# A planner that counts changes of TensorE's tile division and table loads, and orders ready TensorE steps by them

## The chip, the cores and the metric

The kernel runs on one core of a Trainium2 chip. Its engines work side by side, each through its own list of instructions in order, and wait for each other through semaphores: TensorE (PE in the profile, its weight loads PEld), VectorE (DVE), ScalarE (ACT), GpSimd (POOL) and SyncE (SP), which issues most DMAs. The metric is the device time of one execution in microseconds (us). Before the change it is 3449.53 us, the median of three runs (3448.21 to 3455.52).

## What is computed

Six residual blocks act on x, 4 sequences of 1024 tokens with 128 features, all in float32:

```python
x = x + 0.5 * ffn0(layernorm(x))      # 128 -> 512, exact GELU, -> 128
x = x + attn0(layernorm(x))           # 16 heads of 8, scores from squared distances, softmax over 1024
x = x + 0.5 * ffn0(layernorm(x))
x = x + 0.5 * ffn1(layernorm(x))      # two layers, see below
x = x + attn1(layernorm(x))           # 16 heads of 64, causal softmax
x = x + 0.5 * ffn1(layernorm(x))
```

Each layer of `ffn1` shifts half of the features by one token, makes queries, keys and values for 8 heads of 64, normalises and rotates queries and keys, attends locally (each window of 64 tokens sees itself and the window before it), projects and adds to the residual; then it shifts again, takes a layer norm, and runs a gated feed-forward (a value half times GELU of a gate half). The two calls of `ffn1` share their weights.

## The kernel before

**Two passes.** The kernel isn't written as one instruction stream. Its code registers some thousands of small *steps* with `plan.at(t, f, ...)`, each a function with one to a few dozen instructions and a first guess `t` of its time. In a first pass the class `Plan` runs all steps in recording mode: `issue` notes for each instruction its engine and an estimated cost, and `touch` derives which step has to follow which. `order` then simulates the engines with these costs and brings the steps into one order. In the second pass the steps run again in this order and emit the real instructions. Each engine gets its instructions in exactly the planned order (`issue` adds a dependence on the engine's instruction before); the times of the plan themselves leave no trace on the chip, which runs each list as fast as its waits allow. Since one helper line, 223, emits everything, all rows of the profile say L223, and shapes tell the steps apart.

**How the plan is made.** `cost` (276) gives each instruction a duration by engine, operation and size. A TensorE product in float32 streams its columns four times (`4 * n / 2400` us), other types once, with a lower bound by type. A product with at most 64 weight columns whose output starts below the first partition counts 0.04 us. `order` (343) keeps for each engine a list `future` of steps whose predecessors are planned and a heap `ready`, sorted by due time `p`. It takes the engine that can start first and its ready step with the smallest `p`, gives it buffers if it needs them (`places`), and lays its instructions on the engines' clocks: 0.22 us (`X_LAT`) from one engine to another, 0.12 between two VectorE instructions of a step, fixed costs for SP's DMAs. At first `p` is the written time `t`. `latest` (502) then plans backward and finds how late each step may start; this becomes `p`, and `best_order` (554) repeats this six times and keeps the order that ended earliest by its own reckoning. `prepare` (306) puts a barrier between groups of steps that need different ScalarE tables (Exp or GELU). SBUF addresses come from the written times; which of a tag's buffers or PSUM slots a step gets is settled in `order`.

**The steps that matter here**, with the part of TensorE's 128 x 128 array that their products use (rows x weight columns):

- First attention (`attn0`, 807): `score` (975) has two products of 64 x 128 in bfloat16, 512 wide; `exp` (984) is one ScalarE instruction over 128 x 1024; `weigh` (988), for two exponentials, has four products of 128 x 9 with 512 columns to stream, placed beside each other in the array. Preparation of the next batch (transposes, projections) is 128 x 128. There are 512 scores and exponentials and 256 weighings; the exponentials have six buffers, the scores two PSUM slots.
- Causal attention (`attn1`, 1078): `score` (1270), transposes, projections use the whole array; `weigh` (1341) has pairs of products of 128 x 64, 256 wide, in 128 steps. The transposed exponentials that it reads have six buffers.
- Local attention (`ffn1`, 1420): `attend` (1644) registers the steps of one *frame*, 128 tokens through one layer's attention; two layers of 32 frames make 64 for each `ffn1`. `score` (1740) starts with two mask products on the whole array and goes on with 16 products of 64 x 64; `weigh` (1791) has 32 of 128 x 64; all else is 128 x 128. Between score and weighing lie a maximum on DVE, exponentials on ACT, a reciprocal on DVE, a multiplication on POOL (`norm_e`, 1778) and transposes on PE (`turn_e`, 1782). Every four frames the next block's tokens are shifted by DMAs. The gated feed-forward of four blocks is gathered between two table changes.

A float32 product counts twice in the profile: it runs as two passes, each with its weight load.

Of the kernel before, what the change touches and what calls it, by code (L numbers as in the profile page):

```python
# [11 lines left out]
FR = mybir.dt.float32r  # L12
# [35 lines left out]
def free_size(x):  # L48
    return math.prod(x.shape[1:])
# [42 lines left out]
class Plan:  # L92
# [6 lines left out]


    X_LAT, LAT, AHEAD = 0.22, {"D": 0.13, "A": 0.09, "G": 0.09, "S": 0.22}, 0.1
    TRIES = 6

    def __init__(self, ctx, tc):
# [116 lines left out]
    def issue(self, engine, name, args, kw):  # L221
        if not self.recording:
            ins = getattr(engine.engine, name)(*args, **kw)  # L223
            prev = self.last.get(engine.key)
            if prev is not None:
                info = mybir.DependencyInfo(mybir.DependencyClass.NoSync, mybir.DependencyReason.DATA)
                self.tc.add_manual_dep(ins.ins, prev, info, reason="order of the plan")
            self.last[engine.key] = ins.ins.name
            return
        out = [kw["out"] if "out" in kw else args[0]] + ([kw["accum_out"]] if "accum_out" in kw else [])  # L230
        ins = [x for x in (*args, *kw.values()) if isinstance(x, bass.AP) and not any(x is o for o in out)]
        banks = {}
        for write, aps in ((False, ins), (True, out)):
            for x in aps:
                b = self.owner.get(x.tensor.name)
                if b is not None:
                    self.touch(b, x, write)
                    if b.space == "P":
                        banks[b] = True
        if name == "activation" and args[2] in (AF.Exp, AF.Gelu):  # L240
            self.cur.table = args[2]
        self.cur.work.append((engine.key, self.cost(engine.key, name, args, kw, out[0], ins), banks))

    def touch(self, b, x, write):
        row = math.prod(x.tensor.shape[1:])
# [27 lines left out]
        if b.users[-1] is not cur:  # L273
            b.users.append(cur)

    def cost(self, key, name, args, kw, out, ins):

        n = free_size(out)
        if key == "P":
            if name == "transpose":  # L280
                return 0.109 if args[1].dtype == F32 else 0.056
            x, w = args[2], args[1]
            if x.dtype == F32:
                t = 4 * free_size(x) / 2400
            else:
                t = max(free_size(x) / 2400, 0.107 if x.dtype == FR else 0.056)
            row = math.prod(out.tensor.shape[1:])
            return 0.04 if free_size(w) <= 64 and out.offset // row else t + 0.004
        if key == "A":
            extra = sum(isinstance(kw.get(z), bass.AP) for z in ("bias", "scale", "accum_out"))  # L290
            return 0.055 + n / 1200 + 0.093 * extra
# [51 lines left out]
    def order(self):  # L343
# [9 lines left out]
            s.left, s.est, s.state, s.behind = len(s.before), 0.0, 0, []  # L353
        free = dict.fromkeys("PADGS", 0.0)
        future, ready = {z: [] for z in "PADGS"}, {z: [] for z in "PADGS"}
        todo, out, dma = [s for s in self.all if not s.left], [], 0.0

        def places(s):

# [64 lines left out]
        while True:  # L424
# [31 lines left out]
                break  # L456
            z = best[1]
            s = self.all[heapq.heappop(ready[z])[1]]
            if s.buffers:
                found = places(s)  # L460
                if found is None:
                    s.state = 0
                    wait(s)
                    continue
                e = max(t for t, _ in found)
                if e > s.est + 1e-9:
                    s.est = e
                    heapq.heappush(future[z], (e, s.p, s.index))
                    continue
                take(s, found)  # L470
            t, before, last = s.est, z, 0.0
            for j, (e, cost, banks) in enumerate(s.work):
                t = max(t, free[e])
                if e != before:
                    t += self.X_LAT
                for b in banks:
# [1583 lines left out]
```

## Time and profile before

| | us |
|---|---|
| median of 3 runs | 3449.53 |
| profiled execution | 3451.22 |
| span of its instructions | 3449.4 |
| granted TensorE clock, mean | 0.96 of full |
| ACT table loads, 18 | 23.1 |

The page cuts the span into 40 slices and gives each engine's busy share in tenths (9 is 90% or more), and below them the granted TensorE clock:

```profile
PE   8999999888787889789999999999998888888868
PEld 6222222766676767567777777777776666667647
DVE  7433240788768687888888888888888797886874
ACT  6999999467667576547667777777776666776753
POOL 1000000276646464433333333333345664664650
PEclk9999999999899999889999999999999999999989
```

The first attention shows as the run of 9s of PE and ACT at the left (slices 2 to 7), the causal attention as PE's run of 9s in the middle (slices 18 to 30), and the two local stages on either side of it, where PE falls to 7 and 8 and the clock drops in places. Busy PE is modelled: the end of a product includes a tail in which the next one already runs.

### The profile page before, as it was taken

Reading aid. Unit: us, or ns where it says so; the run is one execution under the profiler, and the core shown is the slowest. Engines: PE = TensorE matmul, PEld = TensorE weight load, DVE = VectorE, ACT = ScalarE, POOL = GpSimd, SP = SyncE. Lnnn points to the kernel's source line nnn. Section 1 sums busy time; section 2 is a strip of 40 time slices with the busy share of each in tenths; the row PEclk is TensorE's granted clock in tenths of the full one; section 3 lists DMA queues with packets and bytes.
Section 4 is the critical chain, followed back from the end, with each engine's and each line's share of the span. In section 5 each row is a group of like instructions: output and inputs, shape, how many; then the busy total and the mean of one; then the engine's idle time right before and its main releaser. Section 6 shows DMA issues by size and latency. Waiting matters only on the chain.

```text
span 3449.4 us, 76651 instructions
## 1 busy us (share of the span) xinstructions
PE 3066.5 (89%) x27060; PEld 2178.1 (63%) x27060; DVE 2497.1 (72%) x7673; ACT 2424.1 (70%) x6434; POOL 1351.9 (39%) x1483
## 2 busy tenths in 40 slices
PE   8999999888787889789999999999998888888868
PEld 6222222766676767567777777777776666667647
DVE  7433240788768687888888888888888797886874
ACT  6999999467667576547667777777776666776753
POOL 1000000276646464433333333333345664664650
PEclk9999999999899999889999999999999999999989
DMA  1000000122212121122221222222222221222211
GB/s 38 1 1 1 1 3 13 45 60 49 46 35 51 39 51 33 48 63 46 45 51 42 45 48 46 48 49 46 72 54 54 53 47 35 47 48 46 46 36 28
DMA packets 210677, 138.95 MB, mean 40 GB/s; under 512 B 146596, under 2 KB 165880, under 8 KB 210296
## 3 DMA queue, kind: packets, MB, share of 16 engines
q1 hardware_dynamic: 209576, 133.50, 16.9%
q8 instruction: 216, 3.54, 0.4%
q14 instruction: 165, 1.35, 0.1%
q0 software_dynamic: 720, 0.56, 0.1%
HBM read 19.22 MB, written 2.10 MB: 6 GB/s over the span
## 4 chain that ended last, share of the span: by engine, by line
PE 36%; DVE 25%; issue 3%; SPq 3%; DMA 3%; ACT 2%; POOL 2%; DVEq 0%; ACTq 0%; POOLq 0%
PE wordsP L223 36%; DVE wordsS L223 19%; DVE words L223 4%; SPq L223 3%; DMA wordsS<-wordsS 3%; POOL wordsS L223 2%; ACT wordsS L223 1%; ACT words L223 1%; DVE wordsR L223 1%; POOL words L223 1%; DMA wordsS<-c_rot 0%; ACT wordsR L223 0%; DMA words<-words 0%; DVEq L223 0%; ACT L223 0%
## 5 line engine op out<-in xcount | busy, mean ns | idle before, releaser
L223 PE MATMUL wordsP<-wordsS 128*128 128x128 f32 (+8 forms) x12040 | 1686.1, 334 | 271.8 <-POOL wordsS L223 199.2
L223 PEld LDWEIGHTS wordsP<-wordsS 128*128 128x128 f32 (+3 forms) x10248 | 941.7, 147 | 514.3 <-POOL wordsS L223 263.5
L223 ACT ACTIVATE wordsS<-wordsP,wordsS 128x128 f32<-128x128 f32 (+4 forms) x1952 | 915.6, 490 | 371.4 <-PE wordsP L223 201.1
L223 ACT COPY wordsS<-wordsP 128x512 f32<-128x512 f32 (+4 forms) x1040 | 545.5, 537 | 300.1 <-PE wordsP L223 294.4
L223 PE MATMUL wordsP<-wordsR 128*128 128x512 f32 (+2 forms) x2592 | 722.6, 412 | 29.3 <-DVE wordsR L223 10.7
L223 POOL TENSOR_TENSOR wordsS<-wordsS 128x512 f32<-128x512 f32 (+1 forms) x518 | 539.8, 1057 | 516.0 <-DVE wordsS L223 483.4
L223 POOL TENSOR_SCALAR wordsS<-wordsS 128x640 f32<-128x640 f32 (+7 forms) x512 | 382.4, 750 | 683.8 <-DVE wordsS L223 478.6
L223 DVE TENSOR_REDUCE wordsS<-wordsP 128x1 f32<-128x512 f32 (+4 forms) x1024 | 576.2, 581 | 66.5 <-PE wordsP L223 61.0
L223 PE MATMUL wordsP<-wordsS,words 128*64 128x64 f32 (+3 forms) x6216 | 524.8, 300 | 39.5 <-DVE words L223 17.4
L223 PEld LDWEIGHTS wordsP<-wordsR 128*128 128x128 f32 (+1 forms) x2592 | 457.9, 193 | 132.6 <-DVE wordsR L223 13.3
L223 ACT ACTIVATE wordsS<-wordsP 128x1024 f32<-128x1024 f32 x512 | 485.7, 1028 | 23.1 <-PE wordsP L223 20.7
L223 PE MATMUL wordsP<-words 128*128 128x512 f32 (+3 forms) x1540 | 417.7, 377 | 13.2 <-DMA words<-W_vT 10.6
L223 DVE COPY wordsS<-wordsP 128x512 f32<-128x512 f32 (+4 forms) x444 | 238.5, 550 | 209.7 <-PE wordsP L223 206.0
L223 ACT ACTIVATION_READ_ACCUMULATOR wordsS<-wordsP,wordsS 128x1 f32 x1792 | 387.8, 216 | 0.0
L223 DVE TENSOR_TENSOR wordsS<-wordsP,wordsS 128x256 f32<-128x256 f32 (+3 forms) x560 | 253.8, 461 | 162.1 <-PE wordsP L223 129.0
L223 PEld LDWEIGHTS wordsP<-wordsS,words 128*64 128x64 f32 (+2 forms) x5704 | 307.2, 137 | 99.4 <-issue 46.7
L223 PEld LDWEIGHTS <-wordsS 64*128 64x128 bf16 (+1 forms) x1792 | 124.2, 95 | 367.2 <-issue 341.3
L223 PEld LDWEIGHTS wordsP<-words 128*128 128x128 f32 x1540 | 247.3, 192 | 47.5 <-ACT wordsS L223 12.4
L223 ACT ACTIVATE words<-wordsP 128x512 f32<-128x512 f32 x256 | 150.0, 609 | 152.1 <-DVE words L223 74.7
L223 PE MATMUL wordsP<-words,wordsS 64*64 64x128 f32 (+1 forms) x4672 | 234.8, 284 | 24.0 <-DMA words<-words 21.5
L223 DVE TENSOR_TENSOR wordsS<-wordsS 128x1 f32<-128x1 f32 (+4 forms) x1104 | 236.6, 218 | 25.9 <-ACT wordsS L223 13.0
L223 DVE TENSOR_TENSOR words<-wordsP,wordsS 128x256 f32<-128x256 f32 (+1 forms) x448 | 228.9, 529 | 32.1 <-PE wordsP L223 14.7
(55 smaller groups left out, 2441.2 us busy)
## 6 DMA issues: line engine op xcount, KB each, us to landing
words<-words SPq DMA_DIRECT2D x648, 128.0 KB
wordsS<-words SPq DMA_DIRECT2D x88, 128.0 KB
wordsS<-wordsS SPq DMA_DIRECT2D x48, 128.0 KB
wordsS<-wordsS SPq DMA_DIRECT2D x48, 127.0 KB
wordsS<-c_rot SPq DMA_DIRECT2D x16, 256.0 KB
wordsS<-L_attn_x SPq DMA_DIRECT2D x8, 256.0 KB
words<-wordsS SPq DMA_DIRECT2D x16, 128.0 KB
out_dram<-wordsS SPq DMA_DIRECT2D x8, 256.0 KB
```

The lines of the kernel that those rows point to most:

```text
L223: ins = getattr(engine.engine, name)(*args, **kw)
```

## The change

The plan gets another account of what TensorE's work costs, and a rule of choice:

- `mode` gives each TensorE instruction its division of the array: rows and weight columns, each rounded up to 32, 64 or 128, and whether it is a rounded float32 product. `switch` prices a change of rows or columns at 0.1 us (0.2 if one side is 64 x 128 in rounded float32, which no step here has).
- `cost` scales a product by the share of the array that it uses, in place of the 0.04 us for later column tiles; constants per type change a little (a rounded product of 512 from 0.217 to 0.228 us, a float32 product of 128 from 0.217 to 0.222).
- `order` adds the price of a change where the division changes from one instruction to the next, and 1.3 us (`TABLE`) before the first step that needs another table.
- The rule: when the most urgent ready TensorE step would change the division, the plan looks for ready steps that wouldn't, that are due at most 2.0 us (`SLACK`) after it, and that can start by the time it could; if there are any, the most urgent of these goes first.

What the steps do is the same.

```diff
+    SLACK, TABLE = 2.0, 1.3
...
-        self.cur.work.append((engine.key, self.cost(engine.key, name, args, kw, out[0], ins), banks))
+        mode = self.mode(name, args) if engine.key == "P" else None
+        self.cur.work.append((engine.key, self.cost(engine.key, name, args, kw, out[0], ins, mode), banks, mode))
...
-    def cost(self, key, name, args, kw, out, ins):
+    @staticmethod
+    def mode(name, args):
+
+        if name == "transpose":
+            return 128, 128, False
+        tile = lambda n: 32 if n <= 32 else 64 if n <= 64 else 128
+        return tile(args[1].shape[0]), tile(free_size(args[1])), args[1].dtype == FR
+
+    def switch(self, old, new):
+
+        if old is None or old[:2] == new[:2]:
+            return 0.0
+        return 0.2 if any(m == (64, 128, True) for m in (old, new)) else 0.1
+
+    def cost(self, key, name, args, kw, out, ins, mode):
...
-            x, w = args[2], args[1]
+            x = args[2]
             if x.dtype == F32:
-                t = 4 * free_size(x) / 2400
+                t = 4 * free_size(x) / 2400 + 0.009
+            elif x.dtype == FR:
+                t = max(free_size(x) / 2400 + 0.015, 0.112)
             else:
-                t = max(free_size(x) / 2400, 0.107 if x.dtype == FR else 0.056)
-            row = math.prod(out.tensor.shape[1:])
-            return 0.04 if free_size(w) <= 64 and out.offset // row else t + 0.004
+                t = free_size(x) / 2400 + 0.003
+
+            return t * mode[0] * mode[1] / 128**2
...
             s = self.all[heapq.heappop(ready[z])[1]]
+            if z == "P" and self.switch(mode, s.work[0][3]):
+
+                same = [(p, k) for p, k in ready[z] if p <= s.p + self.SLACK and not self.switch(mode, self.all[k].work[0][3])]
+                same = [x for x in same if self.all[x[1]].est <= max(free[z], s.est)]
+                if same:
+                    x = min(same)
+                    ready[z].remove(x)
+                    heapq.heapify(ready[z])
+                    heapq.heappush(ready[z], (s.p, s.index))
+                    s = self.all[x[1]]
...
-            for j, (e, cost, banks) in enumerate(s.work):
+            if s.table is not None and s.table != table:
+                t, table = max(t, free[z]) + self.TABLE, s.table
+            for j, (e, cost, banks, m) in enumerate(s.work):
                 t = max(t, free[e])
+                if e == "P":
+                    t, mode = t + self.switch(mode, m), m
                 if e != before:
                     t += self.X_LAT
```

More of the change, by code (lines that the diff above doesn't have):

```diff
@@ L355, in order @@
         future, ready = {z: [] for z in "PADGS"}, {z: [] for z in "PADGS"}
-        todo, out, dma = [s for s in self.all if not s.left], [], 0.0
+        todo, out, dma, mode, table = [s for s in self.all if not s.left], [], 0.0, None, None
         def places(s):
```

## The prediction

> **What bounds the kernel now.** I read first the page's busy times and slices, then the busy times by stage. The stage borders are mine: they are where the mix of instructions changes (GELU feed-forward, first attention, feed-forward, local attention with gated feed-forward, causal attention, local attention again). The table has one row for each stage: its length, the busy time of each engine with its instruction count, the granted TensorE clock, the DMA share and GB/s.
>
> ```profile
> PE 3066.5 (89%) x27060; PEld 2178.1 (63%) x27060; DVE 2497.1 (72%) x7673; ACT 2424.1 (70%) x6434; POOL 1351.9 (39%) x1483
> ...
> 0.00:85.00 85.00, 68.94 (x513) 59.01 (x514) 67.22 (x306) 57.93 (x113) 13.68 (x18) 1.00 0.15 38
> 85.00:600.00 515.00, 494.31 (x3770) 140.35 (x3769) 162.57 (x483) 491.77 (x526) 3.25 (x3) 1.00 0.01 3
> 600.00:690.00 90.00, 75.82 (x503) 64.20 (x501) 66.67 (x243) 42.80 (x82) 23.70 (x26) 0.92 0.17 44
> 690.00:1485.00 795.00, 648.69 (x7028) 526.07 (x7028) 625.73 (x1948) 514.05 (x1711) 451.04 (x441) 0.92 0.20 45
> 1485.00:2600.00 1115.00, 1086.91 (x7929) 829.77 (x7929) 928.92 (x2760) 785.10 (x2242) 400.10 (x547) 0.99 0.22 51
> 2600.00:3449.00 849.00, 691.87 (x7326) 558.69 (x7323) 645.95 (x1938) 532.49 (x1761) 460.14 (x448) 0.93 0.19 44
> ```
>
> The 89% of PE is an average over stages with different limits. In the first attention ACT works 491.8 of 515 us: it is the bound, and 23 us is all that any order can win there. In the causal attention PE works 1086.9 of 1115: 28 us is open. The two local stages, 1644 us together, have no engine at its limit over the stage, so they are where an order could matter. I looked inside one, at PE in time (start, length, instruction, tiles, count, idle time before) and at two 10 us slices of all engines:
>
> ```profile
> 852.31 0.59 PE L223 MATMUL wordsP<-wordsS 128*128 128x512 bf16 x2
> 852.84 1.10 PE L223 MATMUL wordsP<-words,wordsS 64*64 64x128 f32 x32
> 854.69 0.66 PE L223 MATMUL wordsP<-wordsS 128*128 128x128 f32 x4 [0.75 <-POOL wordsS L223]
> 855.69 1.69 PE L223 MATMUL wordsP<-wordsS 128*128 128x128 f32 x12 [0.34 <-POOL wordsS L223]
> 857.22 0.60 PE L223 MATMUL wordsP<-wordsS,words 128*128 128x128 f32 x4
> 857.69 0.66 PE L223 MATMUL wordsP<-wordsS 128*128 128x128 f32 x4
> 858.28 1.41 PE L223 MATMUL wordsP<-wordsS,words 128*64 128x64 f32 x33
> 859.44 2.34 PE L223 MATMUL wordsP<-wordsR 128*128 128x512 f32 x9
> ...
> 862.25 1.10 PE L223 MATMUL wordsP<-words,wordsS 64*64 64x128 f32 x32
> 864.79 1.43 PE L223 MATMUL wordsP<-wordsS 128*128 128x128 f32 x11 [1.44 <-POOL wordsS L223]
> ...
> 700.00:710.00 10.00, 8.98 (x129) 6.61 (x127) 9.02 (x24) 6.98 (x25) 8.33 (x9) 1.00 0.25 56
> 830.00:840.00 10.00, 9.22 (x129) 7.14 (x131) 9.86 (x32) 7.62 (x29) 7.35 (x9) 1.00 0.12 27
> ```
>
> One frame (128 tokens through the local attention) lasts 862.25 - 852.84 = 9.41 us. PE waits for POOL right after each score; DVE has 9.86 of 10 us filled in the slice at 830 and 9.02 in the slice at 700.
>
> **The change, part by part.** No instruction is added or removed. What changes is the order on each engine, through the plan's costs and one rule. So I ask of each edit how far it brings the plan to the trace, and what an engine could win by it.
>
> *Score of the local attention.* Its 16 products cost the old plan 8 x 0.217 + 8 x 0.04 = 2.06 us (4 x 128 / 2400 + 0.004 for the upper half of the output, 0.04 for the lower). The new one takes a quarter of 0.222 for each: 0.89, with 0.1 on entering and on leaving, 1.09. The row says 1.10 with the tail of the last product. So the old plan put about 1 us of work on PE that isn't there, and the wait of 0.75 to 1.44 us after the score is the trace of it: what was planned next isn't ready. *Weighing*, 32 products of 64 columns: old 16 x (0.111 + 0.04) / 2 = 1.2, new 0.93 + 0.2 = 1.13, trace 859.44 - 858.28 = 1.16. Nothing to win.
>
> What does the freed microsecond bring? It is idle time of PE, which isn't the limit of a frame; DVE is. Where DVE has 9.86 of 10 us the gain is nothing. Where it has 9.02, as in the first layer, at most the 0.84 us of difference per frame. There are 2 stages x 32 such frames. Ends: 64 x 0.8 = 51 us gained, or a loss (rivals). The slice shows the wait, not whether another order removes it, since what PE waits for is POOL's result of the same frame, a chain that the change leaves as long as it is. I take about a quarter, 0.22 us: **-14 us**.
>
> The long holes between blocks of four frames stay. In 790 to 800 us PE is busy 1.75 us and DVE 4.47; the waits of that stage give POOL 134.5 us behind the DMAs of the token shift. Neither SP's costs nor POOL's are touched, and the order around them is free to shift either way.
>
> *Score and weighing of the first attention.* For two exponentials the old plan saw PE at 2 x 2 x 0.217 + (0.857 + 3 x 0.04) = 1.85 us against ACT's 2 x 0.908 = 1.82, so it took PE for the limit. The new one sees 2 x (2 x 0.108 + 0.1) + 4 x 0.216 + 0.1 = 1.60 against 1.82, and ACT is the limit, as in the stage table. Preparation for the next batch can then be put where it doesn't hold a score. ACT waits for PE there 20.7 us in 67 waits, the longest 1.8 us. I take a third: **-6 us**; ends -19 and, if a score is put behind, +17 (rivals).
>
> *The rule that keeps the division.* It looks for a ready step of the present division that is due no more than 2.0 us after the step that would change it. The price of a change can be read above: four transposes take 857.69 - 857.22 = 0.47 us to the next start when nothing changes, and 858.28 - 857.69 = 0.59 when 64-column work follows: 0.12 us, beside the 0.1 of the plan. The Trainium skill says in "TensorEngine Tiling (Array Packing)", Key Properties, that a change of the tiling mode drains TensorE. The page gives no price. If that meant waiting out the tail, the first score line would pay it: its pair of mask products lasts 0.59 us, but the score starts 0.53 us after the pair, so no full tail is waited for. By the row the 128 weighings of the causal attention pay 256 x 0.12 = 31 us; priced as a full tail of 0.19 (0.66 - 0.47), 49 us. I use the row. But only neighbours can share a change. 128 weighings in 1115 us lie 8.7 us apart on average, and the local attention's 9.4; a slack of 2.0 us joins few of them. Each join saves 0.24; ten of them 2 us, and a weighing put off takes output, projection and its six buffers with it. Ends -5 and +5, taken as **0**. In the local attention the score step begins with mask products on the full array, so the rule doesn't even see its change.
>
> *Other TensorE costs.* A rounded product of 512 goes from 0.217 to 0.228; nine of them take 2.18 us above (861.62 - 859.44), 0.242 each. A better number, on work that fills PE in any order. 0.
>
> *Table loads.* The ACT rows have 18 of them, 1283 ns each, 23.1 us before and after, since exponentials and GELUs keep their barriers. A rule speaks against the 1.3 us of the plan: "ScalarE: Activation LUTs", What ACT_TABLE_LOAD costs, adds a drain of 1.38 us, 2.66 in all. By that, 18 x 2.66 = 48 us would be spent and the plan would still see half; by the row, which shows 1.1 us idle before all 18, it sees all. Either way only what the plan puts beside a load can move: 18 x 0.1 = 2 us, either sign. 0.
>
> Sum: -14 - 6 = -20 us. The profiled execution took 3451.2 us (3449.4 of span and 1.8 around it), so 3431; from the median of 3449.5 it is 3429.5, and I say **3430**, 0.6% faster.
>
> **Rivals.** *The padding was useful (slower).* Old costs made a local frame about 8.5 us of PE: projection 2.0, transposes 2.1, score and mask 2.5, weighing 1.2, output 0.9. The new ones make it 7.6, while the trace has 9.4, because DVE takes longer than its own costs say. The surplus on PE stood in for what DVE and POOL lack. Without it the plan believes in a faster frame and sets work that waits for DVE and POOL at the head of PE's and ACT's queues, where the ready work behind it has to wait. Its place is the wait after the score, its price the growth of that wait where DVE is held too. At 0.3 us in each of 128 frames it is +38 us, 3488; from 20 / 128 = 0.16 us on it eats the forecast's gain. For it: DVE's 9.86 of 10. Against it: an engine that is full isn't slowed by an order in front of another.
>
> *A score goes behind a second weighing (slower).* In the first attention a score that would change the division yields to a ready weighing. One weighing takes about 0.97 us, of which some 0.3 is covered by the running exponential; 25 of 256 cost 25 x 0.67 = 17 us: 3467 alone. For it: ACT has almost no slack. Against it: a weighing is due when its buffer of six is needed, three exponentials later, which is about the 2.0 us of slack.
>
> *Nothing comes of it.* ACT and PE stand at their limits in two stages and DVE in much of the rest; the rule finds no neighbours. 3449.
>
> **How the numbers follow.** Forecast 0.48, with its own range of 3400 to 3442; padding 0.27; scores behind 0.10; nothing 0.15. A difference of 0.2%, 7 us, is about what a measurement of this kernel can tell from no change. Faster by more: most of the forecast, 0.47. Within: the rest of it and most of the last rival, 0.14. Slower: both slow rivals and a piece of the last, 0.39. The range goes from 3395 (two thirds of the two gains' far ends of 51 and 19 us, and some shuffle) to 3488, the padding rival at its price.
>
> **What would show it.** Right: PE's wait for POOL in the two local stages (122.0 + 125.6 us on the weight loads) falls, DVE's 9.02 at 700 rises, ACT's wait for PE in the first attention falls below 20.7, the causal stage stays within 10 us of 1115, busy sums stay. Wrong: frames longer than 9.4 us with DVE less full (padding), ACT waits of 0.7 us and more (scores behind), or a local stage that changes by more than 30 us through its block borders, which I hold to be outside the plan's reach.

## The result, and the profile after

The changed kernel takes 3460.83 us (median of 9 runs, 3456.19 to 3463.04) against 3450.55 us for the kernel before in 9 runs beside it: ratio 1.0028, 95% interval 1.0018 to 1.0039. It is 0.28% slower, where 0.6% faster was forecast. The profiled execution took 3458.93 us with a span of 3457.2, 7.8 us longer than before. Below is the page's first row (busy time, share of the span, instructions), and then the busy times by stage, in the columns of the table shown for the kernel before and at the same places of the program (the first stage left out).

```profile
PE 3060.1 (89%) x27060; PEld 2164.3 (63%) x27060; DVE 2535.6 (73%) x7673; ACT 2424.1 (70%) x6434; POOL 1356.9 (39%) x1483
```

```profile
86.00:608.00 522.00, 493.76 (x3762) 138.15 (x3761) 162.64 (x481) 493.52 (x524) 3.26 (x3) 1.00 0.01 3
608.00:705.00 97.00, 79.06 (x527) 66.55 (x526) 71.53 (x251) 46.95 (x97) 30.75 (x33) 0.93 0.22 56
705.00:1500.00 795.00, 650.36 (x7013) 520.87 (x7013) 649.31 (x1947) 510.32 (x1701) 448.21 (x436) 0.93 0.19 44
1500.00:2609.00 1109.00, 1077.62 (x7941) 826.28 (x7942) 913.51 (x2763) 786.89 (x2249) 399.44 (x548) 0.99 0.22 51
2609.00:3457.00 848.00, 689.73 (x7311) 552.64 (x7307) 670.84 (x1928) 527.78 (x1755) 461.60 (x446) 0.93 0.19 44
```

Three things stand in these rows. The first attention, ACT's stage, lasts 522 us instead of 515 with the same work. The causal stage is shorter. And VectorE, with the same 7673 instructions, is busy 38 us longer (2497.1 before): 48 more in the two local stages (625.7 to 649.3 and 645.9 to 670.8) and 15 less in the causal one. No engine got more work, but something makes its instructions last longer.

Those borders are rounded. The following table takes exact ones, the starts of ACT's 18 table loads, worked out from each trace. With the experiments told below it is what most of this document reads from. The causal column begins with the causal attention and ends inside the second local stage; the last one is the rest of that stage and the end. Its sum is the span.

| kernel | start, first feed-forward | first attention | second feed-forward | first local stage | causal and on | rest | span |
|---|---|---|---|---|---|---|---|
| before | 84.6 | 512.8 | 89.6 | 825.1 | 1393.1 | 544.2 | 3449.4 |
| after | 85.2 | 521.8 | 95.2 | 827.7 | 1382.6 | 544.6 | 3457.2 |
| e1, after without the rule | 85.3 | 521.8 | 95.2 | 825.0 | 1395.2 | 542.7 | 3465.3 |
| e2, before with the rule alone | 87.4 | 512.5 | 88.6 | 819.9 | 1387.6 | 542.3 | 3438.5 |
| e3, after, first score at full cost | 85.2 | 513.6 | 95.0 | 825.4 | 1381.3 | 545.8 | 3446.3 |
| e4, before, first score at half cost | 84.8 | 526.4 | 88.3 | 825.7 | 1393.5 | 546.1 | 3464.6 |
| e8, before, local score at true cost | 85.2 | 512.8 | 94.0 | 798.6 | 1380.9 | 543.7 | 3415.3 |
| e10, e2 and e8 together | 87.1 | 511.3 | 94.6 | 798.0 | 1372.0 | 544.1 | 3407.1 |

From before to after: +9.0 in the first attention, +5.6 in the feed-forward behind it, +2.6 in the first local stage, -10.5 in the causal column, +1.0 in the rest, 7.8 in sum. With such a mix of signs a single cause is unlikely, so each place was tried by itself.

### The profile page after: what moved, and what is told of

Read it like the earlier page. It is cut to its first block, busy times and chain, and to the rows that moved or that the text cites. A ratio compares the mean times of both kernels' runs of the same rounds, so it can differ in the third digit from the quotient of the medians.

```text
span 3457.2 us, 76620 instructions
## 1 busy us (share of the span) xinstructions
PE 3060.1 (89%) x27060; PEld 2164.3 (63%) x27060; DVE 2535.6 (73%) x7673; ACT 2424.1 (70%) x6434; POOL 1356.9 (39%) x1483
## 4 chain that ended last, share of the span: by engine, by line
PE 45%; DVE 33%; ACT 7%; DMA 5%; issue 4%; SPq 4%; POOL 1%; DVEq 0%; ACTq 0%; POOLq 0%
PE wordsP L225 45%; DVE wordsS L225 26%; ACT wordsS L225 6%; DVE words L225 6%; SPq L225 4%; DMA wordsS<-wordsS 4%; DVE wordsR L225 1%; ACT words L225 1%; POOL wordsS L225 1%; DMA words<-W_kT 0%; DMA wordsS<-c_rot 0%; POOL words L225 0%; DMA wordsS<-L_ffn_k_scale 0%; ACT wordsR L225 0%; DMA words<-L_ffn_w 0%
## 5 line engine op out<-in xcount | busy, mean ns | idle before, releaser
L225 PEld LDWEIGHTS wordsP<-wordsR 128*128 128x128 f32 (+1 forms) x2592 | 455.6, 192 | 134.5 <-DVE wordsS L225 19.7
L225 ACT ACTIVATE wordsS<-wordsP 128x1024 f32<-128x1024 f32 x512 | 489.1, 1023 | 28.5 <-PE wordsP L225 27.6
L225 DVE TENSOR_TENSOR wordsS<-wordsS 128x1 f32<-128x1 f32 (+4 forms) x1104 | 246.8, 230 | 26.3 <-ACT wordsS L225 18.5
L225 DVE SCALAR_TENSOR_TENSOR wordsS<-wordsS 128x17 f32<-128x17 f32 (+5 forms) x818 | 246.1, 305 | 7.2
```

## Experiments: the first attention's 9 us

Two edits reach this stage: the cost of a score (two products of 64 x 128 go from 0.217 to 0.108 us each in the plan) and the rule, which might put a score behind a second weighing. e1 switches off the rule, e2 keeps nothing but the rule, e3 gives the score its old cost within the changed kernel, and e4 puts the halved cost alone into the kernel before.

e1 (against after):

```diff
-            if z == "P" and self.switch(mode, s.work[0][3]):
+            if False and self.switch(mode, s.work[0][3]):
```

> The changed plan with the rule off, costs and prices kept. Theory A (halving the score's cost takes the pacing out of the first attention): the first attention, from its table load to the next one, stays near 522 us (before 512.8, after 521.8). Theory B (the rule puts scores behind same-division steps): it goes back to about 513. If the 10.5 us won from the causal attention on came from joined weighings, that stretch goes from 1382.6 back to about 1393 and the whole to 3467 under A; if from the costs, it stays near 1383 and the whole near 3460.

Measured: 3469.83 us, ratio to before 1.0049 (1.0036 to 1.0062). The first attention stays at 521.8: the rule isn't what lengthens it. The causal column goes back to 1395.2.

e2 (against after; the costs of before return, price and table load are zero, so only the rule is left):

```diff
-    SLACK, TABLE = 2.0, 1.3
+    SLACK, TABLE = 2.0, 0.0
...
-            return t * mode[0] * mode[1] / 128**2
+            row = math.prod(out.tensor.shape[1:])
+            return 0.04 if free_size(w) <= 64 and out.offset // row else t + 0.004
...
-                    t, mode = t + self.switch(mode, m), m
+                    mode = m
```

> The plan of before with its own costs and the rule alone, no price for a change of division or a table. Theory A: first attention near 513 us; theory B: near 522. If the rule's joined weighings made the gain of the causal stretch, it is near 1383 here, otherwise near 1393. The whole: 3440 if the rule brings that gain alone, 3450 if it brings nothing, 3460 or more if it is what costs.

Measured: 3442.41 us, 0.9967 (0.9955 to 0.9980). With the rule and the old costs the first attention is where it was before (512.5), and the causal attention, from its first to its last weighing, keeps 9.9 of the 10.6 us that it gained (1094.3 before, 1084.4 here, 1083.7 after).

e3 (against after):

```diff
-            return t * mode[0] * mode[1] / 128**2
+            return t * (1 if mode[:2] == (64, 128) else mode[0] * mode[1] / 128**2)
```

> The changed plan, but a product of 64 x 128 costs the whole array's time again (0.216 instead of 0.108 us), which concerns the score of the first attention alone. Theory A: the first attention goes from 521.8 to about 513 us, the rest stays within a few us of the changed kernel, the whole near 3452. Theory B: the first attention stays near 522, the whole near 3460.

Measured: 3451.77 us, 0.9997 (0.9989 to 1.0006): one number put back takes 8.2 us out of the first attention (513.6) and leaves the other columns within 3 us.

e4 (against before):

```diff
-            return 0.04 if free_size(w) <= 64 and out.offset // row else t + 0.004
+            return 0.04 if free_size(w) <= 64 and out.offset // row else (t + 0.004) * (0.5 if w.shape[0] == 64 and free_size(w) == 128 else 1)
```

> The plan of before with one cost changed: the score of the first attention at half (0.108 us). Theory A: the first attention goes from 512.8 to about 522 us and the whole to about 3459. Theory B: it stays near 513, the whole near 3450.

Measured: 3469.33 us, 1.0044 (1.0031 to 1.0057), and 526.4 us in the first attention, with every other column within 2 us of before. The cause of the 9 us is shown from both sides: it is the halved cost of the score. In all runs together, the five kernels with it need 521.8 to 526.4 us for this stage and the 15 without it 511.3 to 518.5.

How it works is to be seen in ACT's timeline, the same 12 us of the stage in both kernels (start, length, instruction, count, and the idle time before with what ended it). First before, then after:

```profile
249.60 4.93 ACT L223 ACTIVATE wordsS<-wordsP 128x1024 f32<-128x1024 f32 x5
254.75 1.94 ACT L223 ACTIVATE wordsS<-wordsP 128x1024 f32<-128x1024 f32 x2 [0.22 <-PE wordsP L223]
257.02 5.72 ACT L223 ACTIVATE wordsS<-wordsP 128x1024 f32<-128x1024 f32 x6 [0.33 <-PE wordsP L223]
```

```profile
249.73 1.94 ACT L225 ACTIVATE wordsS<-wordsP 128x1024 f32<-128x1024 f32 x2 [0.28 <-PE wordsP L225]
251.91 1.94 ACT L225 ACTIVATE wordsS<-wordsP 128x1024 f32<-128x1024 f32 x2 [0.23 <-PE wordsP L225]
254.08 1.94 ACT L225 ACTIVATE wordsS<-wordsP 128x1024 f32<-128x1024 f32 x2 [0.23 <-PE wordsP L225]
256.25 1.94 ACT L225 ACTIVATE wordsS<-wordsP 128x1024 f32<-128x1024 f32 x2 [0.24 <-PE wordsP L225]
258.46 1.94 ACT L225 ACTIVATE wordsS<-wordsP 128x1024 f32<-128x1024 f32 x2 [0.27 <-PE wordsP L225]
```

After, every pair of exponentials waits for PE, and PE's timeline of that window says for what:

```profile
249.56 0.62 PE L225 MATMUL wordsP<-wordsS,words 128*128 128x128 bf16 x8
250.12 1.69 PE L225 MATMUL wordsP<-wordsS 64*128 64x512 bf16 x12
251.74 0.62 PE L225 MATMUL wordsP<-wordsS,words 128*128 128x128 bf16 x8
252.29 1.69 PE L225 MATMUL wordsP<-wordsS 64*128 64x512 bf16 x12
253.91 0.62 PE L225 MATMUL wordsP<-wordsS,words 128*128 128x128 bf16 x8
```

The lines with 12 products are two scores with one weighing between them (the timeline joins what is alike; the products of 128 x 9 are in it), and between any two of them lies a run of preparation for the next batch, 8 products of 128 x 128. A pair then takes 252.29 - 250.12 = 2.17 us of PE, which has no gap, while ACT needs 1.94. Written as letters, S a score, W a weighing, p a run of preparation, PE's order from the 200th piece on is (worked out from the traces)

```
before  SpSWSSWSpSWSSWSpSWSSWSpSWSSWSpSWSSWSpSWSSWSpSWSSpWSSWSpSWSSWSpSWSSpWSSpW
after   SSWSSWSSWSSWSpSWSSWSSWSpSWSpSWSpSWSpSWSpSWSpSWSpSWSpSWSpSWSpSWSpSWSpSWSp
```

Of the some 120 runs of preparation, 4 stand behind the run ahead of them with only `SWS` between in the kernel before; in the changed one 97, in e1 97, in e4 99, in e3 and e2 at most 2. A pair with a run needs 2.17 us on the chip where ACT needs 1.94. The stretches without preparation can't make up for that, since ACT is the limit in them and only two PSUM slots hold scores.

The new plan didn't take these pairs for cheaper than they are. The pair itself takes 251.74 - 250.12 = 1.62 us of PE in the rows above, as the new cost says (1.60), and by the planner's own reckoning (worked out with the planner of each kernel) a pair with its run lasts 2.14 us in the new plan. It reckons 509.0 us from the first exponential to the last, where the chip takes 518.7; the old plan reckoned 535.3, where the chip takes 509.7. So the old plan expected PE to be the limit and spread the preparation thin, which suited ACT on the chip; the new one is closer to the chip and still lines the runs up. Why its due times put them in a row isn't settled. ACT's waits for PE in the stage (us in all, times, longest) say it in one line each: 20.7 in 67 waits before, and after

```profile
ACT wordsS L225 <- PE wordsP L225: 27.6, 103, 1.9
```

and in e3 and e4

```profile
ACT wordsS L225 <- PE wordsP L225: 21.2, 66, 1.9
```

```profile
ACT wordsS L223 <- PE wordsP L223: 30.7, 112, 1.9
```

## Experiments: the rule in the causal attention

The time from the first to the last weighing of the causal attention was read in all 20 kernels: the 9 with the rule need 1080.6 to 1089.5 us (mean 1084), the 11 without it 1084.5 to 1104.0 (mean 1093). e1 against the changed kernel is the clean pair, 1094.5 against 1083.7. The ranges meet, though: two kernels without the rule are at 1084.5 (e14) and 1089.6 (e17, a mere nudge of before, told below). Three more runs turn the rule's and the table's settings. e5 and e6 are e2 with another slack:

```diff
-    SLACK, TABLE = 2.0, 0.0
+    SLACK, TABLE = 1.0, 0.0
```

> The rule alone as in e2, with a slack of 1 us instead of 2. In the planned order 126 runs of weighings stand in the causal attention, as against 127 before and 111 in e2: hardly one is joined, though steps are put in another order. If joined weighings make the gain, the time from the first to the last weighing of the causal attention is near 1094 us (before 1094.3, e2 1084.4) and the whole near 3452; if putting weighings off is what helps, some of the gain is there, and the whole is between 3442 and 3448.

```diff
-    SLACK, TABLE = 2.0, 0.0
+    SLACK, TABLE = 8.0, 0.0
```

> The rule alone as in e2, with a slack of 8 us. 106 runs of weighings stand in the causal attention. If joined weighings make the gain at some 0.6 us each (9.9 us for 16), it comes to 1081 us from the first to the last weighing; if each is worth only the 0.2 us of two changes, to 1083 at best. Steps put off by up to 8 us can cost more than that in any stage: then the whole is above e2's 3442.

e7 is the changed kernel with no cost for a table load:

```diff
-    SLACK, TABLE = 2.0, 1.3
+    SLACK, TABLE = 2.0, 0.0
```

> The changed plan without the 1.3 us for a table load; all else kept. If the planned table load is what makes the second feed-forward longer (from its table load to the next one 89.6 us before, 95.2 after), it comes back to about 89 and the whole to about 3455; if it is the other costs, it stays near 95 and the whole near 3460. The first attention stays near 522 either way.

Measured: e5 (slack 1) 3442.61 us, 0.9977 (0.9969 to 0.9986), causal attention 1089.5; e6 (slack 8) 3446.86, 0.9988 (0.9981 to 0.9994), 1085.3; e7 3448.94, 0.9991 (0.9983 to 1.0000), 1086.5. A slack of 1 us brings about half of the gain, 8 us no more than 2 us does. Without the table's 1.3 us the changed kernel is 12 us faster, but over many places (the last gated stretch of the first local stage -6, the end of the second -4.5), and the second feed-forward keeps its length (96.5).

The rule does join weighings, which the forecast held to be rare. A weighing has two to eight pairs of products (the last pair 128 wide), and each product counts twice. PE's timeline of the changed kernel shows the weighing of two pairs and that of four in one go, 24 rows of 128 x 64 in all:

```profile
2171.21 2.38 PE L225 MATMUL wordsP<-wordsS 128*64 128x256 f32 x24
```

where e1, in the same part of its order, has the one (8 rows), products on the whole array, and then the other (16):

```profile
2174.58 0.87 PE L225 MATMUL wordsP<-wordsS 128*64 128x256 f32 x8
2175.39 0.96 PE L225 MATMUL wordsP<-wordsR 128*128 128x512 f32 x3
2176.19 0.86 PE L225 MATMUL wordsP<-words 128*128 128x512 f32 x4
...
2177.87 1.74 PE L225 MATMUL wordsP<-wordsS 128*64 128x256 f32 x16
```

The 128 weighings stand in 108 separate runs after, in 128 in e1. That is 40 changes of division saved. What one costs can be read from the starts of single products in the trace: the last pairs of a weighing start 0.109 us apart, and the next product on the whole array starts 0.203 us after the last of them, 0.09 more, whichever product it is; on the way in, a weighing behind a float32 product of 128 starts 0.203 us after it, too. At about 0.1 us for a change the 40 are worth 4 of the 10.8 us. The other 6 or 7 aren't settled. They come with another order of the same work: e5 has its 5 us with 126 runs, and e14 reaches 1084.5 with no weighing joined.

## Experiments: the local stages

Here the forecast had its largest term. e8 gives only the local score its true cost, in the kernel before; e10 has the same line in e2, so with the rule.

```diff
-            return 0.04 if free_size(w) <= 64 and out.offset // row else t + 0.004
+            return 0.0555 if w.shape[0] == free_size(w) == 64 else 0.04 if free_size(w) <= 64 and out.offset // row else t + 0.004
```

> The plan of before with one cost changed: a 64 x 64 product, the score of the local attention, at 0.0555 us, so 0.89 us instead of 2.06 for a score. The forecast's main term: 14 us gained in the two local stages (within their stretches between table loads 687.0 and 418.5 us before, without the GELU stretches), the whole near 3439. If DVE bounds the frames: within 5 us of before. The padding rival: 20 us or more lost.

> The rule alone (slack 2 us) together with the local score at a quarter of the array, all other costs as before; no prices, no table. If the two gains stand beside each other (10 us of e2 in the causal attention, 33 us of e8 in the local stages), the whole is near 3408. If e8's gain is the luck of one order, the rule's reshuffle loses it and the whole is 3430 or more.

Measured: e8 3417.17 us, 0.9902 (0.9888 to 0.9915), and e10 3411.03, 0.9885 (0.9871 to 0.9898), the fastest of all, 1.2% below before and 1.4% below the changed kernel. So the edit from which most was hoped seems to bring 33 us alone and nothing within the whole change. By its expectation e10 speaks against luck, but it was no test of it: the rule finds nothing to do in the local stages. In e2 the order of TensorE's products there is that of the kernel before, product by product, and e10 has the same long waits there as e8 (counted below). The next three add one more part of the change each to e8: the price of a change of division (0.1, with no rule), the cost of the local weighing, and nearly the whole of the new constants.

```diff
+                if e == "P":
+                    t, mode = t + self.switch(mode, m), m
```

> e8 (the plan of before with the local score at its true cost) plus 0.1 us for each change of division, no rule, no table. If the price eats the gain, the first local stretch goes from 254.1 back to about 269 us and the whole from 3417 to about 3450; otherwise it stays within 4 us of 254 and the whole near 3417. The first attention stays near 513 (in the planned order its preparation isn't clustered).

```diff
-            return 0.0555 if w.shape[0] == free_size(w) == 64 else 0.04 if free_size(w) <= 64 and out.offset // row else t + 0.004
+            return 0.0555 if w.shape[0] == free_size(w) == 64 else (4 * free_size(x) / 2400 + 0.009) / 2 if w.shape[0] == 128 and free_size(w) == 64 else 0.04 if free_size(w) <= 64 and out.offset // row else t + 0.004
```

> e8 plus the new cost of the 128 x 64 products (half of the whole array's, for both halves, instead of full for one and 0.04 us for the other). If this eats the gain, the first local stretch goes back to about 269 us; otherwise it stays near 254 and the whole near 3417.

```diff
-                t = 4 * free_size(x) / 2400
+                t = 4 * free_size(x) / 2400 + 0.005
...
-                t = max(free_size(x) / 2400, 0.107 if x.dtype == FR else 0.056)
+                t = max(free_size(x) / 2400 + 0.011, 0.108) if x.dtype == FR else free_size(x) / 2400 - 0.001
```

> e8 plus the changed constants of TensorE products: a rounded product of 512 at 0.228 instead of 0.217 us, a float32 product of 128 at 0.222 instead of 0.217. A frame's planned TensorE time grows by about 0.2 us. If this eats the gain, the first local stretch goes back to about 269 us; otherwise it stays near 254 and the whole near 3417.

Measured: e13 3468.26 us, 1.0050 (1.0037 to 1.0062); e14 3441.46, 0.9969 (0.9957 to 0.9981); e15 3458.02, 1.0018 (1.0009 to 1.0027). Each of three small and unlike edits loses most or all of the 33 us, and not at the same places: e13 26 us in the first part of the first local stage (254.1 to 280.2) and 30 in the causal column, e14 12 and 14 at the same two, e15 30 in the causal column. (The price of e13 also lengthens the first attention, to 518.5.) That looked less like three causes than like an order that had fallen well by chance. e17 and e18 put it to the test: the latency between engines in the plan is 0.21 instead of 0.22 us, on before and on e8.

```diff
-    X_LAT, LAT, AHEAD = 0.22, {"D": 0.13, "A": 0.09, "G": 0.09, "S": 0.22}, 0.1
+    X_LAT, LAT, AHEAD = 0.21, {"D": 0.13, "A": 0.09, "G": 0.09, "S": 0.22}, 0.1
```

> The plan of before with a latency of 0.21 instead of 0.22 us between engines, which says nothing new about the chip. If such a nudge moves the whole by less than 5 us, a difference of 10 us between two plans has a reason in their costs; if it moves it by 10 us or more, differences of this size between plans are within the scatter of orders.

> e8 with the same nudge. If the true cost of the local score is what gains, the whole stays within 10 us of 3417 and the local stages keep their sum of holes (61 and 73 us in e8, 92 and 88 before); if e8 is a lucky order, it goes to 3435 or more with holes of 80 us and more in each stage.

Measured: e17 3454.86 us, 1.0008 (0.9999 to 1.0017), and e18 3460.37, 1.0024 (1.0015 to 1.0032). The nudge moves before by 3 us and e8 by 43. By the expectation of e17 the 3 us speak for reasons in the costs, but they are a sum: its second feed-forward is 8.2 us longer, its first local stage 10.1 shorter and its causal column 5.8 longer than before. With the nudge on both, the true cost of the local score makes the kernel 5 us slower; without it, 33 us faster. The gain of e8 is real, but by these four runs it belongs to that one order and not to the edit. All 20 traces together say the same. From the first to the last local score the two stages take 1488.4 us together in the mean of the 8 kernels with the old cost of that score (1480.9 to 1499.8), and 1486.5 in the 12 with the true one; without e8 and e10 it is 1492.7 (1482.3 to 1510.2). (These kernels share much of their orders, so they are fewer than 20 independent cases.)

**What sets e8's order apart** are the holes, most of them at the borders between blocks of four frames. Counted are the times above 2.2 us from one product's start to the next between the first and the last score of each local stage (number and sum, from the traces):

| kernel | first stage | second stage |
|---|---|---|
| before | 14, 92.0 us | 13, 87.9 us |
| after | 13, 87.4 | 11, 88.1 |
| e8 (and e10) | 11, 61.3 | 11, 73.0 |
| e18 | 14, 89.1 | 16, 104.9 |

From before to e8 the holes shrink by 45.6 us, more than the whole gain, and in e13, e14 and e15 they are back by 33 to 41 us. One of them in the changed kernel: first SP's queue, where the shift's third DMA stands, then what VectorE, GpSimd and TensorE do when it ends.

```profile
797.38 6.52 SPq L225 DMA_DIRECT2D wordsS<-wordsS  x1
```

```profile
806.26 0.29 DVE L225 BATCH_NORM_STATS2 wordsS<-wordsS 128x6 f32<-128x128 f32 x1 [2.74 <-DMA wordsS<-wordsS]
806.27 1.26 POOL L225 TENSOR_TENSOR wordsS<-wordsS,words 128x512 f32<-128x512 f32 x1 [11.49 <-DMA wordsS<-wordsS]
806.59 0.18 DVE L225 BATCH_NORM_AGGREGATE wordsS<-wordsS 128x2 f32<-128x6 f32 x1
806.69 0.87 DVE L225 TENSOR_TENSOR wordsS<-wordsS 128x18 f32<-128x18 f32 x1
807.48 0.28 DVE L225 BATCH_NORM_STATS2 wordsS<-wordsS 128x6 f32<-128x128 f32 x1
807.49 2.04 POOL L225 TENSOR_TENSOR wordsS<-wordsS 128x512 f32<-128x512 f32 x2
...
808.58 1.68 PE L225 MATMUL wordsP<-wordsS 128*128 128x128 f32 x6 [9.45 <-POOL wordsS L225]
```

POOL stood idle for 11.49 us before `bias2`, the addition of the feed-forward's bias, which waits for the token shift; behind it in its queue were other products (807.49), and PE waited 9.45 us for POOL. The DMA of 0.8 KB alone stands on SP from 797.38 to 803.90. Over the first local stage POOL's waits for those DMAs (us, times, longest) come to 134.5 us in 8 waits before, and after and in e8 to

```profile
POOL wordsS L225 <- DMA wordsS<-wordsS: 123.7, 7, 26.1
```

```profile
POOL wordsS L223 <- DMA wordsS<-wordsS: 64.8, 6, 25.7
```

The natural theory was that `bias2` at the head of POOL's queue makes the hole (theory C in the expectations that use letters). e9 tells the plan, in the kernel before, that `bias2` can start only 6 us later after the shift than it assumed; e11 does so on e10 and e12 on the changed kernel. e16 lets the plan see the shift's last small DMA land 4 us later, for all that wait for it.

```diff
+                late = s.f is not None and p.f is not None and s.f.__name__ == "bias2" and p.f.__name__ == "shift"
+                p.after.append((s, gap + 6.0 * late))
```

> The plan of before with one latency changed: the addition of the second bias (bias2, on POOL) is planned 6 us later after the token shift that it has to wait for, since the shift's third DMA holds SP for about 6.5 us where the plan counts 0.6. Theory C (the long holes at the block borders of the local stages are bias2 standing at POOL's head, with the normalisations that PE needs behind it): the local stretches lose several of their holes of 7 to 9 us, POOL's wait for the shift's DMAs in the first local stage (134.5 us) falls by more than half, and the whole comes to 3400 to 3430. If the holes are the shift itself, which the next frames need anyway: within 10 us of before, or slower, since bias2 comes later.

> e10 with the later bias2 of e9. If theory C holds and the local score's gain came through the same holes, it is a little better than the better of e9 and e10, near 3390 to 3405; if they add up in full, near 3370.

> The changed plan, all of it, with the later bias2 of e9. If the local score's gain is missing from the changed kernel only because bias2 stands in front of the normalisations at its block borders, the first stretch of the local stage (269.0 us in the changed kernel, 254.1 in e8) comes to 255 or less and the whole to 3420 or less, while the first attention stays at 522. If something else eats the gain, it stays above 265 and the whole above 3445.

```diff
-                    end = dma + 0.96 - self.X_LAT
+                    end = dma + 0.96 - self.X_LAT + (4.0 if cost == 1 * 3 * 64 * 4 / 360e3 else 0.0)
```

> The plan of before with the shift's third DMA (three rows of 64 numbers) planned to land 4 us later, for all that wait for it. If the holes at the block borders are steps planned too early at the heads of POOL's and DVE's queues, the local stretches shorten by 3 us or more for each of some ten borders and the whole comes below 3430; if the frames need the shift at that time anyway, the whole stays within 10 us of before.

Measured: e9 3441.66 us, 0.9975 (0.9965 to 0.9986); e11 3446.14, 0.9987 (0.9980 to 0.9993); e12 3449.28, 0.9996 (0.9988 to 1.0004); e16 3449.69, 0.9998 (0.9989 to 1.0007). The kernel before gains 9 us by it and the changed one 12, but e10 loses 35. With `bias2` later POOL's wait for the shift in the first local stage is 114.8 us, not half of 134.5, and the holes of e9 are still 15 and 14 with 93.9 and 87.1 us, since VectorE's layer-norm statistics wait for the same shift (the first row above); and with the whole shift planned later they are 98.0 and 107.6. So the theory mostly falls: the frames behind the border need the shifted tokens at that time, whoever stands at the head of a queue. Which property of an order makes some borders short stays open.

## Why the forecast was wrong, step by step

**First attention, "-6 us": the step that failed, and in its sign.** The reasoning that ACT is the limit there was right, and so was the cost of 1.60 us for a pair, 1.62 on the chip (where two scores stand side by side, two changes of division are left of its three, so 1.50). What failed is the step from there to "preparation can then be put where it doesn't hold a score". The sum left the preparation out: with a run of it the pair takes 2.17 us on the chip, above ACT's 1.94, and in the new order 97 of some 120 runs come with only one pair between them and the run ahead. The old score cost was wrong by a factor of two and served as pacing. Measured: +9.0 us, ACT's wait 27.6 instead of below 20.7. The slow rival for this stage, a score behind a second weighing, had the right place and size (+17 for 25 cases) but the wrong agent: the rule does nothing there.

**Local score, "-14 us": the wait went, the time didn't.** The named sign came true. PE's gap after a score (start of its last product to the next start, where below 2.2 us) fell from a mean of 0.72 us to 0.28, 0.44 in each of some 112 of the 128 frames, 49 us (in the 8 kernels with the old cost it is 0.53 to 0.75, in the 12 with the true one 0.23 to 0.30); the weight loads' wait for POOL in the first local stage is 87.8 us instead of 122.0:

```profile
PEld wordsP L225 <- POOL wordsS L225: 87.8, 64, 9.8
```

In PE's timeline one frame lasts 882.43 - 874.48 = 7.95 us, where 9.41 was shown before:

```profile
874.48 1.10 PE L225 MATMUL wordsP<-words,wordsS 64*64 64x128 f32 x32
875.51 1.99 PE L225 MATMUL wordsP<-wordsS 128*128 128x128 f32 x16
...
882.43 1.10 PE L225 MATMUL wordsP<-words,wordsS 64*64 64x128 f32 x32
883.46 0.33 PE L225 MATMUL wordsP<-wordsS,words 128*128 128x128 f32 x1
884.49 1.99 PE L225 MATMUL wordsP<-wordsS 128*128 128x128 f32 x16 [0.70 <-POOL wordsS L225]
```

Yet from the first to the last score the two stages, without their holes, take 1316.1 us after and took 1310.8 before, in the mean of the 12 kernels with the true cost 1316.9 and of the 8 others 1302.9. So the term of -14 us measures about nothing with the holes and some +14 without them; the frames did get longer, as the padding rival said, but not at the place that it named. What grew in place of PE's wait is VectorE's time. The rows of its smallest two-input instructions, by shape, before and after (count, busy, mean ns, idle before):

```profile
L223 DVE SCALAR_TENSOR_TENSOR wordsS<-wordsS 128x17 f32<-128x17 f32 x368 | 80.1, 218 | 9.4
L223 DVE TENSOR_TENSOR wordsS<-wordsS 128x17 f32<-128x17 f32 x276 | 60.4, 219 | 6.2
```

```profile
L225 DVE SCALAR_TENSOR_TENSOR wordsS<-wordsS 128x17 f32<-128x17 f32 x368 | 118.2, 321 | 3.8
L225 DVE TENSOR_TENSOR wordsS<-wordsS 128x17 f32<-128x17 f32 x276 | 82.3, 298 | 2.7
```

The same 17 columns take 218 ns on average before and 321 after. They didn't become more work, they wait for GpSimd: in the hole shown above the two-input instruction at 806.69 lasts 0.87 us and ends at 807.56, as POOL's from 806.27 does (807.53). Of the 826 two-input instructions with 17 or 18 columns, 66 last over 0.4 us before and 183 after, and every one of them starts beside an instruction of POOL and ends within 0.15 us of one's end. Over all of VectorE, what its instructions that start beside a POOL instruction take above their shape's usual time is about 210 us before and 280 after: 70 us, against the 49 that PE's waits gave. In e2 and e4, which lack the local score's cost, those sums are about 210 and 205; in e1 and e8, which have it, about 275 and 290. The Trainium skill describes it in "SBUF — State Buffer", section "SBUF: two separate sides": VectorE and GpSimd share a port pair, a lock and not a split of bandwidth, taken for the whole instruction by whichever starts first, a GpSimd one or a VectorE one with two SBUF inputs or in a two-port mode; "the other fully blocks". The rows agree: the end of POOL's instruction sets theirs. So the forecast's "DVE has 9.86 of 10 us filled" counted waiting as work, and a tighter order only moved PE's wait to VectorE. e8 has as much of it as the changed kernel: its gain is in the holes. The named sign that VectorE's share would rise came true in this empty way: 649.3 of 795 us in the first local stage, where it was 625.7. Two slices of the changed kernel have it at 9.28 and at the full 10.00, with PE at 8.3:

```profile
740.00:750.00 10.00, 8.25 (x103) 6.48 (x102) 9.28 (x26) 7.47 (x28) 7.15 (x8) 1.00 0.31 67
845.00:855.00 10.00, 8.33 (x103) 6.66 (x103) 10.00 (x35) 8.02 (x27) 7.83 (x10) 1.00 0.16 36
```

That this lock is what ate the shorter waits is read from these traces and not tried: no run took POOL's instructions out of the way.

**The rule, "0": mis-sized.** It was the one part whose gain stayed wherever it was tried, about 10 us in the causal attention. The averages of 8.7 us between weighings hid that the ready list often holds a second one within 2 us: 20 joins instead of "few". At the 0.2 us for two changes that the starts show, beside the forecast's 0.24, that is 4 us, so the price was near and the count wrong. The rest comes with the other order and isn't explained.

**Borders, "outside the plan's reach": wrong.** Edits of the plan's costs do move them, by 46 us from before to e8 and back by 60 with e18. In the changed kernel they happened to stay (180 before, 175 after).

**Constants and table loads, "0".** Without the table's cost the changed kernel is 12 us faster (e7), and with the constants e8 is 41 us slower (e15). Of the 41 us, 33 lie in the holes of the local stages; of the 12, most lie in the second local stage outside its holes (733 us from first to last score after, 724 in e7). A nudge moves stages by as much, so the runs don't show a price of their own; but the forecast's 0 and its 2 us either way left this out. The drain that the forecast weighed beside the table loads isn't seen: in the changed kernel 15 of the 18 loads, 1.283 us each, start within 0.02 us of ACT's instruction ahead and have the next one 0.01 us behind them.

**What held.** Busy PE stayed within 7 us, and the causal stage of the windows is 1109 us, within the 10 of 1115 that were named, though the rule moved it. "Padding was useful" was right as a principle, and in the first attention, but its own place, the wait after the local score, shrank instead of growing. (Its parts of an old frame add up to 8.7 us, not 8.5.) "Nothing comes of it" was near in its number by luck, as a sum of parts of 10 us of both signs. By its own reckoning the planner takes 3127.0 us before and 3080.1 after: a plan that is 47 us shorter became a kernel that is 10 us longer. The +5.6 us of the second feed-forward come with the local score's cost (94.0 in e8, 93.9 in e14, 88.3 to 88.6 in e2 and e4) but also with the mere nudge of e17 (97.8); why isn't settled.

## What to carry to other kernels

A wrong cost in a planner may be doing a job: before mending it, ask which engine it kept ahead of another. Here the score at its old cost gave 8 us back within the changed kernel (e3), and the rule with all old costs is faster than either (e2). A busy engine in the profile may be waiting inside its instructions: compare one shape's mean time with its shortest before calling an engine the limit. And where a static order has a few long holes, a change of 0.01 us in one assumed latency can move its time by 43 us, or its stages by 10 us each way while the sum hardly moves. So an edit is judged by the stage it touches and by nudged copies of both kernels, not by one order of each.

## What the hardware showed that was not expected

- A VectorE instruction over 17 or 18 columns, 0.18 us in the median, lasts up to 1.33 us in the changed kernel beside a GpSimd instruction of 1.0 to 1.3 us.
- The third DMA of the token shift, 3 pieces of 256 bytes, stands on SP's queue for 6.52 us in the row above, behind two DMAs of 512 and 508 pieces of 256 bytes that stand there for 0.79 and 0.76 us; the plan counts 0.6 us for it. What it waits for there was not tried.
- A change of division costs about 0.1 us in the causal attention: 0.203 us from a weighing's last start to the next product's, where 0.109 lies between its own last starts. That is the plan's price, and near the 0.12 read before.
